# Where the finished batch's last operations, the bounds' check, the heads of attn2 and the first embedding sums stand in a two-layer attention kernel

## The chip, the core and the metric

The kernel runs on one core of a Trainium2 chip. The metric is device time in microseconds (us) of one execution; three executions of the kernel before gave 2773.93, 2775.44 and 2777.14 us, so the median is 2775.44 us. The engines are named as the profile names them: PE is the matrix engine (TensorE), DVE the vector engine, ACT the scalar engine, POOL is GpSimd, and SP is the sync engine, which here does nothing but issue DMAs.

## What is computed

Everything is float32. The input x has shape (2, 512, 64, 32): two batches of 2048 tokens (S) with 512 channels (C).

```
# layer 0: attention with 8 heads of 64; q and k also see a position embedding
q, k = concat(x, emb) @ Wq, concat(x, emb) @ Wk      # emb: 32 rows of (h), 32 rows of (w)
v    = x @ Wv
x    = x + softmax(q k^T / 8) v @ Wout + bout
# layer 1: Nystrom attention, 256 landmarks (means of 8 tokens), on the normalised tokens
t = tokens(x);  q, k, v = norm(t) @ Wqkv
attn1 = softmax(q kL^T); attn2 = softmax(qL kL^T); attn3 = softmax(qL k^T)
Z   = pinv(attn2)                                     # 6 iterations
t   = t + (attn1 (Z (attn3 v)) + conv33(v)) @ Wout1 + bout1
# feed-forward: two linear maps, folded in the kernel into one 512x512 map mT
t   = t + norm(t) @ mT
```

The kernel computes softmax without subtracting a maximum, which is safe while every score stays under a bound. It therefore also computes bounds of the scores (`bound`, 128 x 24) and, from them, a flag `bad`; if the flag is set, a general path runs after the fast one. With these inputs only the fast path runs.

## The kernel before, in words

PE, DVE, ACT and POOL each run their instructions in the order in which the program writes them (`manual_schedule`, for these four engines). An instruction that waits holds up everything behind it on its engine. The DMA queue of SP is not in this list: a scheduler orders it. So the order in the Python text is the schedule, and where PE would wait, other work is woven in by Python generators. A generator does one unit of work and then yields; `advance(list)` (L792 on) takes one unit from the first generator of a list; a unit that yields `GAP` makes `advance` pass on, so that a gap is a call in which that generator gives PE nothing more.

**Start (L820 to L855, L857 on).** The weights and x are loaded; 20 matmuls warm PE up (L847). For each pair of heads (`Heads0`, 4 pairs for each batch) the embedding's part of q (and of k) is one small matmul (L880), copied by DVE (L882) and spread by one POOL addition to a tile `e` of 128 x 2048 (L884). Each of the four token blocks of 512 is then projected by four matmuls (L896) and added to `e` by DVE (L899). Projections use two PSUM banks in turn (tag `pp`).

**Layer 0 (to about 1430 us).** Attention of pair after pair, with the next pair's projections as filler.

**Between the layers (about 1430 to 1755 us).** Layer 0's output of batch 1 is finished (`out0`, `norm0`), while the keys, queries and landmarks of layer 1 are made for batch 0 and then for batch 1 (`others`, `keys_and_queries`, L1230 to L1255). Between them stands, for each pair of heads, `attend` (attn2: matmuls L1271, exponential L1278 on ACT, normalisation L1282 to L1288 on DVE) and `gram` (L1298). For the first three pairs, `attend` takes one PSUM tile of two banks for both heads, `scs`, and gives head h the half `scs[:, h, :]`; from the fourth pair on it takes a bank for each head. `start_scale` (L1178 on) makes a number from all attn2 for the inversion, with a reduction across partitions on POOL.

**The pair loop (about 1755 to 2600 us).** `todo` holds the eight pairs, those of batch 1 first (n = 0 to 3), then those of batch 0 (n = 4 to 7). For pair n, `pinv` runs five iterations; each has two squarings of M and two of R, one for each head (flip L1513, copied by ACT L1514; products L1523; DVE sums L1536). After iteration c it calls `chunk(c)`: attn1 of the pair before (scores L1580, exponential L1585, sum L1589, values L1596, row sums L778, reciprocal L1609; the reciprocals are spread to rows by eight DMAs, L789; `attn1_end`, L1616 on DVE and L1617 on POOL, takes them up in the next chunk), attn3 of the pair after, and, between, `advance(finish)`. Then three small products follow, each a chain from PE (L1498) to ACT (L1502) to PE (L1507) to DVE (L1536), and `last(i)`, i = 0 to 5, fills the holes in these chains. All values matmuls of attn1 write one PSUM bank (tag `av1`), which `attn1_end` reads.

**The finished batch's end (`finish1_units`).** Once batch 1 has all its heads, its four token blocks t go through `Finish1`: load of the block x1 (four DMAs, L1628), four `out` units (four matmuls L956, residual sum L963 on DVE), the normalisation (`norm_units`, `statistics`), and four `map` units (L1673; DVE L1662, L1663; DMA to the output). The normalisation's steps are: sums of channels (DVE L974, L975); mean on PE (L978) and subtraction (DVE L979, 128 x 2048); squares (three ACT instructions, L982, L985) and their sums (three DVE instructions, L987, L988); variance on PE (L991), square root (ACT L993) and reciprocal (DVE L1641). The block's tile `xr` exists once: the next block's load waits for the output DMAs of the block before. In the kernel before, the generator is put into `finish` after pair 4, and so is first advanced in pair 5:

```
        pair.pinv(chunk, last)
        if n == NPAIR:
            finish.append(finish1_units(1, [p.o for p in todo[:NPAIR]]))
```

**The end (about 2600 us on).** attn1 of pair 7 (`last_attn1`) and what is left of `finish` are woven with the first units of batch 0's own four blocks by a string, one letter a unit: f advances `finish`, 1 is attn1, a and b the `out` units of blocks 0 and 1, s and t their normalisations. Then come the bounds' check, and the four blocks' maps, which take the banks `av1`, `pr`, `av3`, `pr`:

```
    for c in "f1f1f1f1f1f1f1fa1a1a1as11bs1bs1bbt":
...
    todo[-1].attn1_end(NTB - 1)
    drain(outs[1])
    next(st[0])
```

The check is one matmul (L2049) with a matrix `halves` (three POOL memsets, L2045 to L2047, in one of three row buffers, tag `rinv`), three small DVE instructions (L2051 to L2054) and a reduction on POOL (L2055). The tiles for batch 0's own blocks (`fs`, loads L1628) take the buffers in which the heads' outputs `o` of batch 1 stood (tag `qo`).

Of the kernel before, what the change touches and what calls it, by code (L numbers as in the profile page):

```python
# [663 lines left out]
def fast_path(  # L664
# [145 lines left out]
    def gap(n=1):  # L810
        for _ in range(n):
            yield GAP
# [5 lines left out]


    emb_sb = wpool0.tile([64, H + W], F32, name="emb_f")  # L820
    nc.vector.memset(emb_sb, 0.0)
    w_sb = {kind: wpool0.tile([P, KC, C], F32, name=f"w{kind}_f") for kind in "qk"}
    we = {kind: wpool0.tile([64, C], F32, name=f"we{kind}_f") for kind in "qk"}

    def load_w0(kind, cols, queue=nc.sync):
        w = {"q": wq0, "k": wk0}[kind]
        nc.sync.dma_start(w_sb[kind][:, :, cols], chunked(w[:C, cols]))
        queue.dma_start(we[kind][:, cols], w[C:, cols])

    nc.gpsimd.dma_start(emb_sb[:32, :H], freq)  # L830
    nc.gpsimd.dma_start(emb_sb[32:, H:], time)
    load_w0("q", slice(0, P), nc.scalar)

    def load_x(src, b, name, first=0, n=NTB):
        tiles = []
# [21 lines left out]
    class Heads0:  # L857
# [13 lines left out]
        def embedded_and_projected(self, kind):  # L871

            cols, xbs = self.cols, self.xbs
            if kind == "q":
                self.q = qopool.tile([P, S], F32, tag="qo", name=f"q_{self.name}")

            def embedded(kind):

                fp = bank(f"fp_{kind}_{self.name}")
                nc.tensor.matmul(fp[:, : H + W], lhsT=we[kind][:, cols], rhs=emb_sb, start=True, stop=True)  # L880
                ft = wpool0.tile([P, H + W], F32, tag="ft", name=f"ft_{kind}_{self.name}")
                nc.vector.tensor_copy(ft, fp[:, : H + W])  # L882
                e = wpool0.tile([P, H, W], F32, tag="e", name=f"e_{kind}_{self.name}")
                nc.gpsimd.tensor_tensor(  # L884
                    e,
                    ft[:, :H].unsqueeze(2).to_broadcast([P, H, W]),
                    ft[:, H:].unsqueeze(1).to_broadcast([P, H, W]),
                    ALU.add,
                )
                return e.rearrange("p h w -> p (h w)")  # L890

            def project(kind, dst, e, t):
                toks = slice(t * TB, (t + 1) * TB)
                pp = bank(f"pp_{kind}_{self.name}_{t}")
                for k in range(KC):
                    nc.tensor.matmul(  # L896
                        pp, lhsT=w_sb[kind][:, k, cols], rhs=xbs[t][:, k, :], start=k == 0, stop=k == KC - 1
                    )
                nc.vector.tensor_tensor(dst[:, toks], pp, e[:, toks], ALU.add)  # L899

            dst = self.q if kind == "q" else self.k
            e = embedded(kind)
            yield
            yield GAP
            for t in range(NTB):
                project(kind, dst, e, t)
                yield
# [60 lines left out]
    def deviation(name):  # L968
        return apool.tile([P, TB], F32, tag="rstd", name=f"rstd_{name}", bufs=1)

    def statistics(xb, xn, part, name, squares, row):


        nc.vector.tensor_tensor(part, xb[:, :2, :], xb[:, 2:, :], ALU.add)  # L974
        nc.vector.tensor_tensor(part[:, 0, :], part[:, 0, :], part[:, 1, :], ALU.add)  # L975
        yield
        mean = bank(f"mean_{name}")
        nc.tensor.matmul(mean, lhsT=mean_w, rhs=part[:, 0, :], start=True, stop=True)  # L978
        nc.vector.tensor_tensor(xn, xb, mean.unsqueeze(1).to_broadcast([P, KC, TB]), ALU.subtract)  # L979
        yield  # L980
        sq, *others = squares()
        nc.scalar.activation(sq, xn[:, :2, :], AF.Square)  # L982
        n = 2 // len(others)
        for i, other in enumerate(others):
            nc.scalar.activation(other, xn[:, 2 + i * n : 2 + (i + 1) * n, :], AF.Square)  # L985
            to = sq[:, i * n : (i + 1) * n, :]
            nc.vector.tensor_tensor(to, to, other, ALU.add)  # L987
        nc.vector.tensor_tensor(sq[:, 0, :], sq[:, 0, :], sq[:, 1, :], ALU.add)  # L988
        yield
        var = bank(f"var_{name}")  # L990
        nc.tensor.matmul(var, lhsT=mean_w, rhs=sq[:, 0, :], start=True, stop=True)  # L991
        rstd = row()
        nc.scalar.activation(rstd, var, AF.Sqrt, bias=eps, scale=1.0)  # L993
        yield rstd
# [204 lines left out]
    class Pair:  # L1199
# [59 lines left out]
        def attend(self):  # L1259

            i, L = self.i, self.L
            scs = scores_bank(f"sc2_{i}") if i + 1 < NPAIR else None
            X = self.X = [zpool.tile([P, 2, LM + 1], F32, tag=f"M{h}", name=f"X_{i}_{h}") for h in range(2)]
            rs = small.tile([P, 4], F32, tag="rs2", name=f"rs2_{i}")
            for h in range(2):
                nc.gpsimd.memset(X[h][:, :, LM:], 1.0)
            for h in range(2):
                rows_h = slice(h * D, (h + 1) * D)
                sc = scs[:, h, :] if scs is not None else bank(f"sc2_{i}_{h}")
                for t in range(2):  # L1270
                    nc.tensor.matmul(  # L1271
                        sc[:, t * LM : (t + 1) * LM],
                        lhsT=L[0][rows_h, t * P : (t + 1) * P],
                        rhs=L[1][rows_h, :],
                        start=True,
                        stop=True,
                    )
                nc.scalar.activation(X[h][:, :, :LM], sc.rearrange("p (t n) -> p t n", n=LM), AF.Exp)  # L1278
# [340 lines left out]
    class Finish1:  # L1619
# [10 lines left out]
        def out_units(self):  # L1630
            return residual_units(self.b, self.t, self.xb, self.os, wo_sb, b1_sb, self.name)

        def steps(self, row):
            def squares():
                sq = apool.tile([P, 2, TB], F32, tag="acc", name=f"sq_{self.name}")
                return sq, *(row_of(f"sq{k}_{self.name}").unsqueeze(1) for k in (2, 3))

            self.xn = self.xn()
            for rstd in statistics(self.xb, self.xn, self.xn[:, :2, :], self.name, squares, row):
                if rstd is not None:  # L1640
                    nc.vector.reciprocal(rstd, rstd)  # L1641
                    self.rstd = rstd
                yield

        def norm_units(self):
            steps = self.steps(lambda: deviation(self.name))
            next(steps)
            yield GAP
            next(steps)
            yield  # L1650
            next(steps)
            yield from gap(2)
            next(steps)
            yield
# [28 lines left out]
    def finish1_units(b, os):  # L1683
        for t in range(NTB):
            xb = block_of(lpool, "xr", f"xb_g_{b}_{t}")
            f = Finish1(b, t, os, xb, lambda: block_of(lpool, "xn", f"xn_g_{b}_{t}"))
            yield from f.out_units()
            yield from f.norm_units()
            yield from f.map_units(lambda m, name: bank(name))
# [184 lines left out]
            next(first, None)  # L1874
    drain(first)
    todo[1].prefetch_w()
    vals = [values(1)]
    advance(vals)
    for n in todo[NPAIR - 1].front():
        advance(vals, n // 2)  # L1880
    start_scale()
    todo[0].prefetch1(kvpool.tile([P, S], F32, tag="k", name="q2_first"))


# [2 lines left out]
    for n, pair in enumerate(todo):  # L1887
# [20 lines left out]
        def chunk(c):  # L1908
            nonlocal landmarks
            if before and 0 < c <= n_ones:  # L1910
                before.attn1_end(c - 1)
            advance(finish)
            if c == NTB:
                if after:
# [64 lines left out]
        landmarks = start = None  # L1979
        n_ones = NTB if n + 2 < len(todo) else NTB - 1  # L1980
        pair.pinv(chunk, last)
        if n == NPAIR:
            finish.append(finish1_units(1, [p.o for p in todo[:NPAIR]]))

    def last_attn1():
        pair, ended = todo[-1], []
        for t in range(NTB):
            for j in range(2 if t else 0):
                pair.attn1_scores(t, j)
                if ended:  # L1990
                    pair.attn1_end(ended.pop())
                yield
            pair.attn1_add(t)
            pair.attn1_values(t)
            yield
            pair.attn1_sums(t)
# [31 lines left out]
    st = [f.steps(deviation_of(t)) for t, f in enumerate(fs)]  # L2028

    ones_last = last_attn1()  # L2030
    for c in "f1f1f1f1f1f1f1fa1a1a1as11bs1bs1bbt":
        if c == "f":
            advance(finish)
        else:
# [3 lines left out]
    todo[-1].attn1_end(NTB - 1)  # L2038
    drain(outs[1])
    next(st[0])  # L2040

    n = 3 * B * NPAIR

    halves = row_of("halves_f")[:, :P]
    nc.gpsimd.memset(halves, 0.0)  # L2045
    nc.gpsimd.memset(halves[:D, :D], 1.0)
    nc.gpsimd.memset(halves[D:, D:], 1.0)  # L2047
    bp = bank("bp_f")
    nc.tensor.matmul(bp[:, :n], lhsT=halves, rhs=bound, start=True, stop=True)  # L2049
    ok = small.tile([P, n], F32, name="ok_f")  # L2050
    nc.vector.tensor_scalar(ok, bp[:, :n], SAFE, None, ALU.is_lt)  # L2051
    oks = small.tile([P, 1], F32, name="oks_f")
    nc.vector.tensor_reduce(oks, ok, AX.X, ALU.min)
    nc.vector.tensor_scalar(oks, oks, -1.0, 1.0, ALU.mult, ALU.add)  # L2054
    nc.gpsimd.partition_all_reduce(bad, oks, P, bass_isa.ReduceOp.max)  # L2055

    for t in range(NTB):
        maps = fs[t].map_units(wide_banks, 1 if t + 1 < NTB else 2)
        if t + 1 < NTB:
# [96 lines left out]
```

## Time and profile before

| What | us |
|---|---|
| median of three runs | 2775.44 |
| the profiled execution, its own time | 2775.64 |
| its span, first to last instruction | 2773.8 |
| PE busy | 2712.4 |
| DVE busy | 1638.7 |
| ACT busy | 905.8 |
| POOL busy | 197.2 |
| 1400 to 1580 us: span, PE busy | 180.0, 173.0 |
| 2222 to 2604 us: span, PE busy | 382.0, 364.7 |
| 2604 to 2677 us: span, PE busy | 73.0, 62.2 |

The profile covers one execution. Its page gives each engine's busy time, and other views list the instructions in order of time with the idle time ahead of them and what ended it ("<-"). Lines of code stand as L and a number. A line of a view in order of time begins with the start and the length of a group of like instructions. The share of the TensorE clock that was granted is recorded apart; in most of the span it is 1, and in eight stretches within it 0.5.

### The profile page before, as it was taken

Reading aid. Unit: us, or ns where it says so; the run is one execution under the profiler, and the core shown is the slowest. Engines: PE = TensorE matmul, PEld = TensorE weight load, DVE = VectorE, ACT = ScalarE, POOL = GpSimd, SP = SyncE. Lnnn points to the kernel's source line nnn. Section 1 sums busy time; section 2 is a strip of 40 time slices with the busy share of each in tenths; the row PEclk is TensorE's granted clock in tenths of the full one; section 3 lists DMA queues with packets and bytes.
Section 4 is the critical chain, followed back from the end, with each engine's and each line's share of the span. In section 5 each row is a group of like instructions: output and inputs, shape, how many; then the busy total and the mean of one; then the engine's idle time right before and its main releaser. Section 6 shows DMA issues by size and latency. Waiting matters only on the chain. (4 is left out here: it accounts for less than half of the span.)

```text
span 2773.8 us, 41257 instructions
## 1 busy us (share of the span) xinstructions
PE 2712.4 (98%) x17010; PEld 1365.7 (49%) x17010; DVE 1638.7 (59%) x2076; ACT 905.8 (33%) x1352; POOL 197.2 (7%) x133
## 2 busy tenths in 40 slices
PE   9999999999999999999999999999999999999898
PEld 5343443434343334343344455777677766555334
DVE  3768787774557765747657444544644545556455
ACT  1344343433335244435412223233332323221210
POOL 1101101010001200100002000000000000000000
PEclk9999999999999999999999999999999999999999
DMA  3000000201111200012025532313111202111301
GB/s 115 12 9 9 13 6 7 69 24 50 32 50 54 80 9 7 8 49 64 24 87 186 201 118 92 97 34 115 54 36 58 81 9 90 38 66 31 106 32 47
DMA packets 110358, 157.22 MB, mean 57 GB/s; under 512 B 16065, under 2 KB 67793, under 8 KB 107601
## 3 DMA queue, kind: packets, MB, share of 16 engines
q1 hardware_dynamic: 105664, 137.68, 15.7%
q0 software_dynamic: 4416, 16.79, 1.6%
q8 instruction: 135, 2.21, 0.4%
q14 instruction: 63, 0.51, 0.1%
q10 hardware_dynamic: 80, 0.03, 0.0%
HBM read 82.48 MB, written 55.19 MB: 50 GB/s over the span
## 5 line engine op out<-in xcount | busy, mean ns | idle before, releaser
L1075 DVE TENSOR_TENSOR acc_f<-acc_f,p_f 128x1024 f32<-128x1024 f32 x448 | 589.4, 1316 | 235.6 <-ACT p_f L1065 207.0
L1065 ACT ACTIVATE p_f<-sc_f 128x1024 f32<-128x1024 f32 x512 | 496.4, 1021 | 561.9 <-PE sc_f L1057 550.4
L1057 PE MATMUL sc_f<-q_f,k_f 64*64 64x512 f32 x4096 | 491.7, 595 | 2.4 <-ACT p_f L1065 2.4
L1087 PE MATMUL av_f<-p_f,v_f 64*64 64x512 f32 x4096 | 484.3, 589 | 0.0
L1087 PEld LDWEIGHTS av_f<-p_f,v_f 64*64 64x64 f32 x4096 | 156.5, 133 | 283.0 <-issue 283.0
L1057 PEld LDWEIGHTS sc_f<-q_f,k_f 64*64 64x64 f32 x4096 | 144.8, 133 | 280.9 <-issue 256.0
L1230 PE MATMUL pp<-xh,w 128*128 128x512 f32 x512 | 233.0, 608 | 0.7 <-ACT q L1233 0.7
L1230 PEld LDWEIGHTS pp<-xh,w 128*128 128x128 f32 x512 | 96.5, 194 | 123.2 <-issue 116.0
L1523 PE MATMUL pb<-R 128*128 128x192 f32 (+1 forms) x640 | 151.4, 383 | 1.6 <-DVE M L1536 1.6
L1523 PE MATMUL pa<-M 128*128 128x192 f32 (+1 forms) x640 | 150.6, 380 | 0.0
L941 PEld LDWEIGHTS vp_f<-wv_f,x 128*128 128x128 f32 x1024 | 115.6, 192 | 12.7 <-issue 11.0
L941 PE MATMUL vp<-w,xh 128*128 128x128 f32 x1024 | 120.8, 276 | 0.0
L941 PEld LDWEIGHTS vp<-w,xh 128*128 128x128 f32 x1024 | 117.0, 192 | 7.2 <-issue 4.2
L1523 PEld LDWEIGHTS pb<-R 128*128 128x128 f32 x640 | 107.8, 192 | 25.2 <-DVE M L1536 2.3
L896 PE MATMUL pp_q_f<-x,wq_f 128*128 128x512 f32 x256 | 115.9, 606 | 2.9 <-DMA x<-in_x_dram 1.5
L941 PE MATMUL vp_f<-wv_f,x 128*128 128x128 f32 x1024 | 118.5, 276 | 0.0
L1523 PEld LDWEIGHTS pa<-M 128*128 128x128 f32 x640 | 108.0, 193 | 21.0 <-ACT M L1514 2.5
L956 PE MATMUL yp_g<-o,wo_f 128*128 128x512 f32 x256 | 115.5, 598 | 0.8 <-DVE y_g L1662 0.8
L956 PE MATMUL yp_f<-q_f,wo_f 128*128 128x512 f32 x256 | 114.0, 598 | 2.2 <-issue 1.2
L1673 PE MATMUL fp_g<-xn_g,mT 128*128 128x512 f32 (+1 forms) x264 | 115.7, 589 | 0.0
L896 PE MATMUL pp_k_f<-x,wk_f 128*128 128x512 f32 x256 | 114.1, 599 | 0.4 <-DVE q_f L899 0.4
L1105 POOL TENSOR_TENSOR q_f<-q_f,rinv_f 128x512 f32<-128x512 f32 x32 | 45.9, 1434 | 920.4 <-DMA rinv_f<-acc_f 920.4
(196 smaller groups left out, 2762.0 us busy)
## 6 DMA issues: line engine op xcount, KB each, us to landing
xh<-xh_fd SPq DMA_DIRECT2D x12, 1024.0 KB, 5.4
rinv_f<-acc_f SPq DMA_DIRECT2D x256, 32.0 KB, 1.9
xr_f<-in_x_dram SPq DMA_DIRECT2D x8, 1024.0 KB, 5.2
x_fd<-xr_f POOLq DMA_DIRECT2D x8, 1024.0 KB, 4.6
xh_fd<-xn_f POOLq DMA_DIRECT2D x8, 1024.0 KB, 4.6
k_fd<-k SPq DMA_DIRECT2D x32, 256.0 KB, 2.8
q_fd<-q SPq DMA_DIRECT2D x32, 256.0 KB, 2.9
xb_g<-x_fd SPq DMA_DIRECT2D x32, 256.0 KB, 4.3
```

The source lines that it names most:

```text
L896: nc.tensor.matmul(pp, lhsT=w_sb[kind][:, k, cols], rhs=xbs[t][:, k, :], start=k == 0, stop=k == KC - 1)
L941: nc.tensor.matmul(vp[:, j * P : (j + 1) * P], lhsT=xb[:, k, j * P : (j + 1) * P], rhs=w_of(k), start=k == 0, stop=k == KC - 1,)
L956: nc.tensor.matmul(yp, lhsT=wo_sb[:, k, m * P : (m + 1) * P], rhs=oTs[k][:, toks], start=k == 0, stop=k == NPAIR - 1,)
L1057: nc.tensor.matmul(sc[r * D : (r + 1) * D, h, :], lhsT=hd.k[rows, lo : lo + D], rhs=hd.q[rows, t * TB : (t + 1) * TB], start=True, stop=True,)
L1065: nc.scalar.activation(p, sc, AF.Exp, scale=D**-0.5)
L1075: nc.vector.tensor_tensor(acc, first if c == 1 else acc, p, ALU.add)
L1087: nc.tensor.matmul(av[r][half, :], lhsT=hd.v[keys, c, half], rhs=pp[keys, h, :], start=c == 0, stop=c == NST - 1,)
L1105: nc.gpsimd.tensor_tensor(o, o, rinv, ALU.mult)
L1230: nc.tensor.matmul(pp, lhsT=self.w[j][:, c, :], rhs=xhs[t][:, c, :], start=c == 0, stop=c == KC - 1)
L1523: nc.tensor.matmul(dst, lhsT=lhsT[:, k, t * P : (t + 1) * P], rhs=rhs[:, k, :], start=k == 0, stop=k == 1)
L1673: nc.tensor.matmul(fp[:, cols], lhsT=mT[:, k, m * P : (m + 1) * P], rhs=self.xn[:, k, cols], start=k == 0, stop=k == KC - 1,)
```

## The change

It has six parts.

1. The queue of a first weight's DMA becomes that of its caller, so that the first columns of Wq and their embedding rows go out from ACT's queue, followed there by the two embedding tables, which POOL's queue issued before. The memset of the table's tile covers only the two blocks that no DMA fills. The embedding sums of the very first pair (q and k) run on DVE.
2. `statistics` can stop between the squares (ACT) and their sums (DVE): `apart`. The finished batch's `norm_units` use it, and place their gaps differently; each block also begins with two gaps after its load.
3. The finished batch's generator is put into `finish` in pair 4, chunk 1.
4. `attend` takes a buffer of its own for each head of the first three pairs, and its memsets of the ones column run on DVE.
5. The string of the last stage is another, and `last_attn1` adds its exponentials one unit earlier.
6. The bounds' check stands ahead of and around `start_scale`, between the layers.

```diff
-    nc.vector.memset(emb_sb, 0.0)
+    nc.vector.memset(emb_sb[:32, H:], 0.0)
+    nc.vector.memset(emb_sb[32:, :H], 0.0)
...
-        nc.sync.dma_start(w_sb[kind][:, :, cols], chunked(w[:C, cols]))
+        queue.dma_start(w_sb[kind][:, :, cols], chunked(w[:C, cols]))
         queue.dma_start(we[kind][:, cols], w[C:, cols])
-    nc.gpsimd.dma_start(emb_sb[:32, :H], freq)
-    nc.gpsimd.dma_start(emb_sb[32:, H:], time)
     load_w0("q", slice(0, P), nc.scalar)
+    nc.scalar.dma_start(emb_sb[:32, :H], freq)
+    nc.scalar.dma_start(emb_sb[32:, H:], time)
...
-                nc.gpsimd.tensor_tensor(
+                engine = nc.gpsimd if self.b or self.hp else nc.vector
+                engine.tensor_tensor(
                     e,
...
-    def statistics(xb, xn, part, name, squares, row):
+    def statistics(xb, xn, part, name, squares, row, apart=False):
...
             nc.scalar.activation(other, xn[:, 2 + i * n : 2 + (i + 1) * n, :], AF.Square)
+        if apart:
+            yield
+        for i, other in enumerate(others):
             to = sq[:, i * n : (i + 1) * n, :]
             nc.vector.tensor_tensor(to, to, other, ALU.add)
...
-            scs = scores_bank(f"sc2_{i}") if i + 1 < NPAIR else None
+            scs = [scores_bank(f"sc2_{i}_{h}")[:, 0, :] for h in range(2)] if i + 1 < NPAIR else None
...
-                nc.gpsimd.memset(X[h][:, :, LM:], 1.0)
+                nc.vector.memset(X[h][:, :, LM:], 1.0)
...
-                sc = scs[:, h, :] if scs is not None else bank(f"sc2_{i}_{h}")
+                sc = scs[h] if scs else bank(f"sc2_{i}_{h}")
...
         def norm_units(self):
-            steps = self.steps(lambda: deviation(self.name))
+            steps = self.steps(lambda: deviation(self.name), True)
+            next(steps)
+            yield from gap(2)
+            next(steps)
+            yield
             next(steps)
             yield GAP
-            next(steps)
-            yield
             next(steps)
             yield from gap(2)
             next(steps)
...
             f = Finish1(b, t, os, xb, lambda: block_of(lpool, "xn", f"xn_g_{b}_{t}"))
+            yield from gap(2)
             yield from f.out_units()
...
+    halves = row_of("halves_f")[:, :P]
+    nc.gpsimd.memset(halves, 0.0)
+    nc.gpsimd.memset(halves[:D, :D], 1.0)
+    nc.gpsimd.memset(halves[D:, D:], 1.0)
     vals = [values(1)]
     advance(vals)
     for n in todo[NPAIR - 1].front():
         advance(vals, n // 2)
+    n_bounds = 3 * B * NPAIR
+    bp = bank("bp_f")
+    nc.tensor.matmul(bp[:, :n_bounds], lhsT=halves, rhs=bound, start=True, stop=True)
+    ok = small.tile([P, n_bounds], F32, name="ok_f")
+    nc.vector.tensor_scalar(ok, bp[:, :n_bounds], SAFE, None, ALU.is_lt)
...
     start_scale()
+    nc.gpsimd.partition_all_reduce(bad, oks, P, bass_isa.ReduceOp.max)
...
                 before.attn1_end(c - 1)
+            if n == NPAIR and c == 1:
+                finish.append(finish1_units(1, [p.o for p in todo[:NPAIR]]))
             advance(finish)
...
-        if n == NPAIR:
-            finish.append(finish1_units(1, [p.o for p in todo[:NPAIR]]))
...
         pair, ended = todo[-1], []
+        pair.attn1_add(0)
...
                     pair.attn1_end(ended.pop())
+                if j:
+                    pair.attn1_add(t)
                 yield
-            pair.attn1_add(t)
             pair.attn1_values(t)
...
-    for c in "f1f1f1f1f1f1f1fa1a1a1as11bs1bs1bbt":
+    for c in "11fff11f1ff1aaffff1f1f1f1faas11bs1bs1bbt":
...
-    halves = row_of("halves_f")[:, :P]
...
-    nc.gpsimd.partition_all_reduce(bad, oks, P, bass_isa.ReduceOp.max)
```

More of the change, by code (lines that the diff above doesn't have):

```diff
@@ L1631, in out_units, with steps @@
             return residual_units(self.b, self.t, self.xb, self.os, wo_sb, b1_sb, self.name)
-        def steps(self, row):
+        def steps(self, row, apart=False):
             def squares():
@@ L1638, in steps @@
             self.xn = self.xn()
-            for rstd in statistics(self.xb, self.xn, self.xn[:, :2, :], self.name, squares, row):
+            for rstd in statistics(self.xb, self.xn, self.xn[:, :2, :], self.name, squares, row, apart):
                 if rstd is not None:
@@ L1880, in fast_path @@
         advance(vals, n // 2)
+    n_bounds = 3 * B * NPAIR
[3 more added lines that the diff above has]
+    nc.vector.tensor_scalar(ok, bp[:, :n_bounds], SAFE, None, ALU.is_lt)
+    oks = small.tile([P, 1], F32, name="oks_f")
+    nc.vector.tensor_reduce(oks, ok, AX.X, ALU.min)
+    nc.vector.tensor_scalar(oks, oks, -1.0, 1.0, ALU.mult, ALU.add)
     start_scale()
+    nc.gpsimd.partition_all_reduce(bad, oks, P, bass_isa.ReduceOp.max)
     todo[0].prefetch1(kvpool.tile([P, S], F32, tag="k", name="q2_first"))
@@ L2040, in fast_path @@
     next(st[0])
-    n = 3 * B * NPAIR
-    halves = row_of("halves_f")[:, :P]
[L2045 to L2054, printed above, removed]
-    nc.gpsimd.partition_all_reduce(bad, oks, P, bass_isa.ReduceOp.max)
     for t in range(NTB):
```

## The prediction

> **What bounds the kernel.** The page's first part comes first.
>
> ```profile
> PE 2712.4 (98%) x17010; PEld 1365.7 (49%) x17010; DVE 1638.7 (59%) x2076; ACT 905.8 (33%) x1352; POOL 197.2 (7%) x133
> ```
>
> PE is busy in all but 61.4 us of the span of 2773.8. The change takes no matmul away, so it can win only idle time of PE and matmuls that ran slowly. The view of waits, for PE, names the idle time:
>
> ```profile
> PE p_pb L1513 <- DVE R L1536: 6.9, 2, 6.3
> PE sc L1271 <- ACT X L1278: 6.2, 3, 3.5
> PE rs L778 <- DVE acc L1589: 5.1, 1, 5.1
> PE bp_f L2049 <- POOL halves_f L2047: 4.9, 1, 4.9
> PE mean_g L978 <- DVE xn_g L975: 3.2, 1, 3.2
> PE pp_q_f L896 <- DVE q_f L899: 0.9, 1, 0.9
> ```
>
> The columns are total, times and longest, in us. The second line is attn2, the fourth the bounds' check, the first, third and fifth the finished batch. Next, PE in order of time around attn2 of pair 1 and of pair 3:
>
> ```profile
> 1500.80 1.13 PE L1271 MATMUL sc<-L,L 64*128 64x256 f32 x4
> 1505.40 1.13 PE L1271 MATMUL sc<-L,L 64*128 64x256 f32 x4 [3.47 <-ACT X L1278]
> 1506.46 5.36 PE L1230 MATMUL pp<-xh,w 128*128 128x512 f32 x8
> ...
> 1577.66 1.14 PE L1271 MATMUL sc<-L,L 64*128 64x256 f32 x8
> ```
>
> The second head's matmuls wait until ACT has taken the first head's exponential. Pair 3 has a bank a head, and its eight take 1.14 us without a wait. The eight projections behind the wait take 5.36 us, against 3.70 for the same eight at 1440.78: the view of windows shows why.
>
> ```profile
> 1506.40:1509.80 3.40, 3.40 (x5) 1.51 (x5) 3.33 (x6) 0.60 (x1) 0.86 (x3) 0.50 0.64 242
> 1578.80:1582.00 3.20, 3.20 (x9) 1.52 (x9) 2.93 (x6) 1.09 (x2) 0.00 (x0) 1.00 0.73 251
> ```
>
> The last column but two is the granted clock: 0.50 behind the wait, 1.00 behind pair 3. So a long wait is paid twice. Last, the largest gap, and DVE at the end:
>
> ```profile
> 2402.74 0.48 PE L1513 MATMUL p_pb<-ident,R 128*128 128x128 f32 x1 [6.32 <-DVE R L1536]
> 2403.67 3.78 PE L1523 MATMUL pb<-R 128*128 128x192 f32 x8 [0.45 <-DVE M L1536]
> ```
> ```profile
> 2401.54 0.75 DVE L963 SCALAR_TENSOR_TENSOR xb_g<-yp_g,b_f,xb_g 128x512 f32<-128x512 f32 x1 [9.94 <-DMA xb_g<-x_fd]
> ...
> 2674.10 0.69 DVE L1616 TENSOR_TENSOR rinv<-av,rinv 128x512 f32<-128x512 f32 x1 [0.36 <-DMA rinv<-acc]
> ```
>
> The inversion's matmul waits for DVE, which stands at a residual sum of the finished batch until its block lands.
>
> **What the Trainium skill says.** "TensorE: Matmul & The Clock Gate", Part 1: the clock halves when a free-running window of 3413 ns was idle, and a busy one restores it. The trace agrees in length (slow stretches of 3.4 or 6.8 us, each behind waits), but not that a whole idle window is needed: 0.74 us of visible wait at 1433.6 did it. "GPSIMD Engine Reference", 4.1: two-input sums are about twice as slow as on VectorE. Here POOL's `e` takes 3.62 us and DVE's L979, of the same 128 x 2048, 2.28. "ScalarE: Activation LUTs", What ACT_TABLE_LOAD costs: 1283 ns and a drain; the trace has 1.28 us and shows no drain. "Trainium Kernel Development and Optimization", Key Constraints: queues of several engines share the DMA engines, so spreading issues saves only issue time.
>
> **The parts.**
>
> *Start.* PE ends its warm-up at 7.43 us and starts the embedding at 7.36, so earlier tables win nothing. `e` of q ends at 16.74 on POOL; on DVE it follows the copy at 8.12 and ends at about 10.4, ahead of the first projection (11.45). The 0.94 us wait at 16.59 goes. The 0.40 at 25.05 stays (a bank waits for DVE's 0.69 us drain), and so does most of the 1.46 us wait for x, whose issue moves up by one issue (0.44 us), past nothing else on SP. POOL's queue loses two issues, ACT's gains three ahead of a table load that nothing needs before 43 us. Gain **1.0** (bounds -1.0, if tables on ACT's queue, one 0.5 us issue after another, land after 7.4, since wek took 6.5 us to land, and 1.5).
>
> *attn2.* From first matmul to next projection, the three pairs take 2.93 us (1431.74 to 1434.67), 5.66 and 4.36; pair 3 takes 1.07. Pair 0 saves 1.86 and its slow stretch 1.70 (5.40 - 3.70); pair 2 3.29 and 1.49 (8.62 - 7.13). In pair 1 something else is late: the variance, at 1511.66, needs DVE's sum L988, which ends at 1509.15 in a DVE stream without idle time since 1498. PE would be there at 1505.5. It starts at 1509.3 with the two memsets (0.1 us each on POOL) now on DVE, after a wait of 3.7, and I let a slow stretch (1.7) follow: gain 0.6. Sum **8.9** (5.2 if all stretches stay, 10.6 if none does). Behind the memsets on DVE stand only sums that wait for ACT.
>
> *Bounds' check.* It leaves a wait of 4.95 us. But the next matmul, the first map, writes bank `av1`, which DVE's L1616 reads until 2674.79, waiting for spread DMAs: PE starts at 2674.85 instead of 2677.01. The matmul itself (0.3) is paid earlier, behind `gram` at 1751.6; DVE's three instructions (0.12 + 0.18 + 0.15) delay `start_scale` by 0.5, inside the 3.4 us by which M is ready (1755.25) before PE wants it (1758.62); without that cover they would cost 0.5. The POOL reduction queues behind `start_scale`'s own; POOL has nothing urgent. Gain **1.9** (0 to 3.5). The slow stretch behind this wait (now 3.0) stays.
>
> *Finished batch.* I wrote out every call of `finish` for both kernels: 53 calls before, 69 after, 14 of them in the last string instead of 8. Waits that belong to it, in order of PE: 1.05 (2331.7), 6.32, 0.45, 1.59, 0.26, 0.63, 0.59, 3.24, 0.59, 0.46, 1.06, 0.53, 0.55, 5.06 and 0.78 (2637.2), sum 23.2. After the change:
> - Load of block 1: it is issued in pair 5 with two gaps, and 14 us of PE work ahead of the first sum that needs it, against 2.5 + 3.6 us for output DMA and load. 6.32 and 0.45 go.
> - Mean and squares of block 0 fall at the end of pair 4. DVE's 2.28 us subtraction now precedes `iteration_start`, and ACT's squares (1.06 + 0.61 + 0.61) precede the flip copy of pair 5's first product: the flip copy starts 3.6 us after the scores end, against 1.1 in the trace (2231.87, 2232.97). New wait **2.5**.
> - Variance of block 0, in pair 5 chunk 2: square root, table load back and reciprocal (0.69 + 1.28 on ACT, 3.35 on DVE) lie beside 7 us of scores and values. Nothing.
> - Squares of block 1, pair 6 chunk 3, ahead of a flip copy: 0.4. The chain waits of pairs 5 and 6 (1.05, 1.59, 0.26) go, since maps fill them.
> - Block 2: its load still lands after its first product in pair 7 chunk 0, as now: 1.3. Its mean no longer waits (3.24 goes); products wait for banks 0.35; in chunk 3, without matmuls, its sums (2.07) and the row sums' DMA hold DVE: 1.5.
> - Pair 7's end: 0.46 stays; the third small product has no filler: 0.55.
> - Last string: values of block 1 wait for `av1` (row DMAs, DVE behind L974): 1.4. The variance of block 3 comes straight after two `out` units: residual sum 0.75 and sums 2.07 make 2.9. The row sums of block 0 no longer stand behind squares: 5.06 goes; 0.4 for the rest. 0.78 goes.
> Sum 11.8, gain 11.4. Slow stretches before cost 2.2 (behind 6.32), 2.9 (behind 3.24) and 1.5 (behind 5.06), by the matmuls' excess over like ones; one of 1.7 comes behind the 2.9. Gain 4.9, together **16.3** (9 to 22: waits of 15 and no clock gain less one stretch, or waits of 7 and no stretch).
> Buffers: `sq` is held over two chunks, so sums of attn1 take the other `acc` tile; its spread landed some 19 us earlier (about 2397, 2416). No cost. SP carries the same DMAs; the 16 loads of the last blocks (7.2 us) now wait for `out` units in the string, behind block 0's spread and ahead of block 1's.
>
> **Sum:** 1.0 + 8.9 + 1.9 + 16.3 = 28.1. The profiled execution took 2775.64 (span 2773.8 and 1.8 around it), 0.2 above the median: 2775.44 - 28.1 gives **2747**. About 0.2% (5.5 us) is what a measurement can tell from no change.
>
> **Rivals.**
> - *SP's order* (15%). If those 16 loads are queued ahead of block 0's spread, `av1` comes free 7.2 + 3.5 us later, 11 us, and a slow stretch, 1.7: gain 15.4, **2760**. For it: at 2390 a spread already delayed an output DMA by 4 us. Against: the spread is ready 5 us before the loads.
> - *attn2 gains nothing* (10%): the second head waits not for the shared tile but for ACT's order. Then 8.9 is lost: **2756**. Against it speaks pair 3.
> - *Slower* (9%): DVE and ACT in the pair loop. The 16 normalisation steps of the four blocks stand in order ahead of the inversion's small copies and sums. Now they cost 1.0 each (1.05, 1.59, 0.26, 3.24, 0.59, 5.06, 2.9, 1.5, over 16); I count 0.6 (2.5, 0.4, 0.35, 1.5, 2.9, 1.7). From 2.4 each on (0.6 + 28.1/16) the kernel is slower, from 2.7 on by over 0.2%; at 3.0, half of what 3.24 and its stretch cost, it is **2786**. For it: gaps give such steps no PE work. Against: most chunks have 8 us of other matmuls. At 2.0 to 2.7 it is no change (6%).
>
> **Chances.** Forecast 60%, the others 10, 15, 6 and 9%. Faster 85% (60 + 10 + 15), same 6%, slower 9%. The forecast's own bounds give 2737.6 (gain 1.5 + 10.6 + 3.5 + 22) to 2762.2 (-1.0, 5.2, 0, 9); both rivals on the fast side lie within. All terms at their best is unlikely, so the range is **2739 to 2763**, with some 80%.
>
> **What would show it.** Right: attn2's L1271 as one group of 8 in 1.1 us three times, and clock 1 behind pairs 0 and 2; a wait of about 3.7 at the variance behind pair 1; first map waiting about 3 us for L1616; no wait over 3 us between 2300 and 2600; new waits at the start of pair 5 (flip copy) and at block 3's variance. PE idle time falls from 61 to about 45 us. Wrong: several new waits of over 2 us with slow stretches in pairs 4 to 6, DVE or ACT named; or block 0's spread behind loads on SP.

## The result, and the profile after

The changed kernel takes 2767.59 us, the median of 8 executions (2763.43 to 2769.79); beside it, on the same chip, the kernel before took 2774.51 (8 executions, 2773.41 to 2777.14). The ratio is 0.9974, with a 95% interval of 0.9964 to 0.9984: a gain of 4 to 10 us, not of 28. The forecast was 2747 and its range ended at 2763.

The profiled execution after took 2768.05 us, with a span of 2766.2. In the program text everything has moved by a few lines: L1271 is now L1277, L1596 is L1602, L1616 is L1622, L956 is L959, L1628 is L1634, L1673 is L1681, and the loop's L1513 and L1536 are L1519 and L1542.

The page's first part, of the kernel after:

```profile
PE 2705.5 (98%) x17010; PEld 1362.3 (49%) x17010; DVE 1643.3 (59%) x2095; ACT 906.2 (33%) x1352; POOL 188.5 (7%) x113
```

PE is busy for 6.9 us less with the same 17010 matmuls, so that much comes from matmuls that ran at the full clock. Its idle time, 60.7 us, has hardly moved from 61.4. So idle time that the change took away has come back elsewhere. The view of PE's waits says where (total, times, longest, in us):

```profile
PE av L1602 <- DVE rinv L1622: 13.7, 1, 13.7
PE var_n L997 <- issue: 3.7, 1, 3.7
...
PE fp_g L1681 <- DVE rinv L1622: 3.2, 1, 3.2
PE p_pb L1519 <- DVE R L1542: 3.0, 2, 1.9
PE var_g L997 <- DVE sq_g L994: 2.9, 1, 2.9
...
PE pa L1529 <- ACT M L1520: 1.4, 1, 1.4
...
PE p_pa L1519 <- DVE M L1493: 1.2, 1, 1.2
```

The lines of 6.2, 5.1 and 4.9 us that the prediction showed are gone; of those of 6.9 and 3.2, 3.0 and 0.8 are left. The second, third, fifth and sixth of the lines above are waits that it named (3.7, about 3, 2.9 and 2.5). The first is a single wait of 13.7 us that its sum doesn't have. PE around it, in order of time:

```profile
2588.63 2.04 PE L1586 MATMUL sc<-q,L 64*128 64x512 f32 x8
2604.41 3.68 PE L1602 MATMUL av<-p,u 128*64 128x512 f32 x8 [13.75 <-DVE rinv L1622]
2608.03 1.54 PE L981 MATMUL mean_g<-xn_g,mean_w 128*128 128x512 f32 x2
```

The values' matmul of block 1 in the last string waits until DVE has read the bank of block 0. Behind it the matmuls are slow too: eight in 3.68 us, which take 1.94 at the full clock. DVE, in the same stretch:

```profile
2590.78 0.69 DVE L978 TENSOR_TENSOR xn_g<-xn_g 128x512 f32<-128x512 f32 x1
2603.58 0.69 DVE L1622 TENSOR_TENSOR rinv<-av,rinv 128x512 f32<-128x512 f32 x1 [12.10 <-DMA rinv<-acc]
```

DVE isn't late: it has nothing to do for 12.10 us and waits for the DMAs that spread block 0's reciprocals. So the next view is SP's queue:

```profile
2583.89 3.04 SPq L789 DMA_DIRECT2D rinv<-acc  x5
2587.03 9.60 SPq L1634 DMA_DIRECT2D xb_g<-x_fd  x16
2596.99 2.60 SPq L789 DMA_DIRECT2D rinv<-acc  x3
```

SP issues five of the eight spread DMAs, then the 16 loads of the last four blocks, 0.6 us each, and only then the other three. PE stands still for three small issues. The kernel before had the same loads and no such cut:

```profile
2593.31 1.27 SPq L1628 DMA_DIRECT2D xb_g<-x_fd  x3
2595.07 5.01 SPq L789 DMA_DIRECT2D rinv<-acc  x8
2600.13 7.66 SPq L1628 DMA_DIRECT2D xb_g<-x_fd  x13
```

There it was the loads that were cut in two, and a spread in one piece. For the kernel after, the view of windows agrees (busy us of PE, PEld, DVE, ACT and POOL with instructions in brackets, granted clock, DMA share, GB/s):

```profile
2590.67:2604.42 13.75, 0.01 (x1) 0.04 (x2) 1.62 (x4) 1.19 (x3) 0.02 (x1) 0.67 0.78 265
2604.40:2609.00 4.60, 4.59 (x10) 1.35 (x10) 1.00 (x1) 0.00 (x0) 2.12 (x1) 0.51 0.00 2
```

In the first line PE does nothing, DVE and ACT work for under 2 us each, and the DMA engines are at 0.78: it doesn't tell whether the spread waited for its turn on SP or for a share of DMA engines full of the loads' 4 MB. In the second line the clock is at half.

The attn2 part, by contrast, looks as forecast (PE, pair 0 and pair 1):

```profile
1431.23 1.14 PE L1277 MATMUL sc<-L,L 64*128 64x256 f32 x8
1432.30 3.70 PE L1236 MATMUL pp<-xh,w 128*128 128x512 f32 x8
...
1497.18 1.14 PE L1277 MATMUL sc<-L,L 64*128 64x256 f32 x8
1498.25 3.70 PE L1236 MATMUL pp<-xh,w 128*128 128x512 f32 x8
1505.64 1.31 PE L997 MATMUL var_n<-xr_f,mean_w 128*128 128x512 f32 x2 [3.69 <-issue]
1506.74 5.12 PE L1236 MATMUL pp<-xh,w 128*128 128x512 f32 x8
```

Both heads go as one group of eight, eight projections behind pair 0 take 3.70 us, and behind pair 1 the variance waits 3.69 us, with a slow stretch after it.

### The profile page after: what moved, and what is told of

The parts are those of the page before. It is cut to its first block, busy times and chain, and to the rows that moved or that the text cites. A ratio compares the mean times of both kernels' runs of the same rounds, so it can differ in the third digit from the quotient of the medians.

```text
span 2766.2 us, 41210 instructions
## 1 busy us (share of the span) xinstructions
PE 2705.5 (98%) x17010; PEld 1362.3 (49%) x17010; DVE 1643.3 (59%) x2095; ACT 906.2 (33%) x1352; POOL 188.5 (7%) x113
## 4 chain that ended last, share of the span: by engine, by line
PE 89%; DVE 6%; DMA 2%; ACT 1%; issue 1%; SPq 1%; ACTq 0%; DVEq 0%; POOL 0%; POOLq 0%
PE sc_f L1063 15%; PE av_f L1093 14%; PE pp L1236 8%; PE pb L1529 5%; PE pa L1529 4%; PE vp_f L944 4%; PE vp L944 4%; PE fp_g L1681 4%; PE pp_k_f L899 4%; PE pp_q_f L899 4%; PE yp_g L959 3%; PE yp_f L959 3%; DVE acc_f L1081 2%; PE sc L1358 2%; PE sc L1586 2%; PE av L1602 2%
## 5 line engine op out<-in xcount | busy, mean ns | idle before, releaser
L1681 PE MATMUL fp_g<-xn_g,mT 128*128 128x512 f32 (+1 forms) x264 | 115.9, 589 | 3.2 <-DVE rinv L1622 3.2
L959 PE MATMUL yp_f<-q_f,wo_f 128*128 128x512 f32 x256 | 113.8, 598 | 2.2 <-issue 1.2
L959 PE MATMUL yp_g<-o,wo_f 128*128 128x512 f32 x256 | 114.7, 597 | 0.0
```

What stands on the lines that cost most here:

```text
L959: nc.tensor.matmul(yp, lhsT=wo_sb[:, k, m * P : (m + 1) * P], rhs=oTs[k][:, toks], start=k == 0, stop=k == NPAIR - 1,)
L1681: nc.tensor.matmul(fp[:, cols], lhsT=mT[:, k, m * P : (m + 1) * P], rhs=self.xn[:, k, cols], start=k == 0, stop=k == KC - 1,)
```

## The experiments

The theory: the three parts other than the finished batch's are worth what the prediction said, and the finished batch's gain was eaten by SP's order, which cuts block 0's spread in two. The rivals: the bytes of the loads hold up the spread wherever it is queued; the finished batch's new order costs as much by its own small waits; attn2 or the bounds' check fell short. All medians below are of five or more executions (e9: four), each beside the kernel before on the same chip, whose median was 2774.0 to 2774.3 us in these runs.

**e1: the loads behind the spread.** The blocks' objects, which issue the loads when they are made, are made two units later (`L` in the string makes one):

```diff
-    fs = [last_block(t) for t in range(NTB)]
...
+    def load_block():
+        f = last_block(len(fs))
...
-    for c in "11fff11f1ff1aaffff1f1f1f1faas11bs1bs1bbt":
+    for c in "11LLLLfff11f1ff1aaffff1f1f1f1faas11bs1bs1bbt":
```

> The changed kernel with one difference: the 16 loads of the last four blocks are issued two units later in the program, so that SP queues all 8 spread DMAs of block 0's row sums, then the 16 loads. Nothing else moves on any engine. Theory 1 (SP's order): the wait of 13.75 us at the values' matmul, at 2590.7 in the changed kernel, falls to about 1.4 us, and the slow stretch behind it (the first four values' matmuls 3.68 us instead of 1.94) goes: 13 to 14 us less than the changed kernel's 2767.6, about 2754. Rival (the bytes of the loads, 4 MB, slow the spread's DMAs wherever they stand, or the wait only moves to the residual sums that need the loads): a wait of over 8 us stays between 2585 and 2640, and the time is within 4 us of 2767.6.

Measured: 2753.8 us (2750.26 to 2758.06), ratio 0.9927 (0.9913 to 0.9941). SP's queue and PE in the profile of e1:

```profile
2569.84 17.36 SPq L789 DMA_DIRECT2D rinv<-acc  x15
2587.30 9.35 SPq L1634 DMA_DIRECT2D xb_g<-x_fd  x16
```
```profile
2590.59 1.94 PE L1602 MATMUL av<-p,u 128*64 128x512 f32 x8 [1.56 <-DVE rinv L1622]
...
2604.08 1.36 PE L997 MATMUL var_g<-sq_g,mean_w 128*128 128x512 f32 x2 [2.86 <-DVE sq_g L994]
```

The spread is in one piece (one group here with seven of the spread before it), the wait is 1.56 us, close to the 1.4 of the prediction, and the matmuls behind it run in 1.94 us. The place of 16 issues in SP's list is worth 13.8 us between the medians, half of the whole forecast gain.

**e2: attn2 alone** on the kernel before:

```diff
-            scs = scores_bank(f"sc2_{i}") if i + 1 < NPAIR else None
+            scs = [scores_bank(f"sc2_{i}_{h}")[:, 0, :] for h in range(2)] if i + 1 < NPAIR else None
...
-                nc.gpsimd.memset(X[h][:, :, LM:], 1.0)
+                nc.vector.memset(X[h][:, :, LM:], 1.0)
...
-                sc = scs[:, h, :] if scs is not None else bank(f"sc2_{i}_{h}")
+                sc = scs[h] if scs else bank(f"sc2_{i}_{h}")
```

> The kernel before with attn2's part of the change alone (a bank for each head's scores, the memsets of X on DVE). Theory 1 (the prediction's term): 8.9 us less than before, about 2765.6; PE goes from pair 0's and pair 2's second heads without a wait, and a wait of about 3.7 us for the variance follows pair 1. Rival (attn2 waits for ACT's order, not for the shared tile): within 1 us of before, 2774.5.

Measured: 2765.85 us (2764.67 to 2769.02), ratio 0.9973 (0.9962 to 0.9983): 8.2 us less, against 8.9 forecast. The rival is out. In its profile the wait at L1271 is gone and PE's wait for the variance is there, as 3.69 us.

**e3: the finished batch's part alone** (parts 2, 3 and 5 of the change) on the kernel before.

```diff
...
+            if n == NPAIR and c == 1:
+                finish.append(finish1_units(1, [p.o for p in todo[:NPAIR]]))
...
-    for c in "f1f1f1f1f1f1f1fa1a1a1as11bs1bs1bbt":
+    for c in "11fff11f1ff1aaffff1f1f1f1faas11bs1bs1bbt":
```

> The kernel before with the finished batch's part alone (its load a gap earlier, its squares' sums apart, its start within pair 5's chunks, the order of the last string). The other parts measured so far on the changed kernel's trace take 1.5 us off at the start, 8.7 at attn2 and about 2 at the bounds' check. Theory 1 (this part is worth nothing, since the wait of 13.75 us for the split spread eats what the pair loop won): 2773 to 2779, no gain. Rival (the part wins its 16.3 us as predicted and something else in the sum lost it): about 2758.

Measured: 2778.41 us (2775.22 to 2784.54), ratio 1.0018 (1.0012 to 1.0025): this part, forecast to win 16.3, loses 4.4. Its waits:

```profile
PE av L1599 <- DVE rinv L1619: 13.7, 1, 13.7
```

It is the same wait (this kernel has the lines at L1599 and L1619), so it doesn't come from the parts' meeting.

**e4: start and bounds' check alone** (parts 1 and 6).

```diff
...
-    nc.gpsimd.dma_start(emb_sb[:32, :H], freq)
...
+    nc.scalar.dma_start(emb_sb[:32, :H], freq)
...
     start_scale()
+    nc.gpsimd.partition_all_reduce(bad, oks, P, bass_isa.ReduceOp.max)
```

> The kernel before with the start (tables on ACT's queue, first embedding sums on VectorE) and the bounds' check (moved to the middle of the kernel) alone. Theory 1 (the prediction's terms 1.0 and 1.9): 2.9 us less than before, about 2771.6. Rival (the slow stretch at the first small products is longer with the new start, as in the changed kernel's trace, where it took 6.8 us instead of 3.4, and gives the start's gain back): 0 to 1.5 us less, about 2773.5.

Measured: 2771.71 us (2769.01 to 2776.67), ratio 0.9992 (0.9985 to 0.9999): 2.3 us less, against 2.9 forecast. The interval (0.3 to 4.2 us) doesn't separate the two expectations, and no run separates the start from the bounds' check. The rival's longer slow stretch isn't in this kernel's profile: behind the wait near 921 us the clock stays at 1.

**e8: everything but the finished batch's part** (parts 1, 4 and 6).

> The changed kernel without the finished batch's part: start, attn2 and bounds' check on the kernel before. Theory 1 (the parts add up): 8.2 (attn2 alone, 2774.0 - 2765.85) and 2.3 (start and bounds' check alone) less than before, about 2763.5, which is 4 us less than the whole change: the finished batch's part costs 4. Rival (the parts depend on each other, the attn2 gain falls at the end where the finished batch's new order is needed to keep it): 2766 to 2770, no less than the whole change.

Measured: 2762.65 us (2761.57 to 2764.23), ratio 0.9957 (0.9944 to 0.9971). The parts add up, and the change is some 5 us slower than the same change without its largest part.

**e5: half of the loads ahead.** As e1, but the first two blocks are made where the changed kernel makes all four:

```diff
+    load_block()
+    load_block()
-    for c in "11LLLLfff11f1ff1aaffff1f1f1f1faas11bs1bs1bbt":
+    for c in "11LLfff11f1ff1aaffff1f1f1f1faas11bs1bs1bbt":
```

> Between the changed kernel and e1: SP queues 5 spread DMAs of block 0, then 8 of the 16 loads (blocks 0 and 1), then the last 3 spread DMAs, then the other 8 loads. Theory 1 (each load queued ahead costs its turn on SP, 9.6 us for 16, 0.6 each): the wait at the values' matmul is 13.75 - 8 * 0.6 = about 8.9 us, the slow stretch behind it stays, and the time is 4 to 6 us below the changed kernel's 2767.6, about 2762.5. Rival (it's not the number of loads but that the group of 8 is cut in two, or the landing of one load): the wait stays at 12 to 14 us and the time within 2 us of 2767.6.

Measured: 2760.66 us (2760.36 to 2764.64), ratio 0.9956 (0.9942 to 0.9969). SP's queue and PE:

```profile
2584.18 3.89 SPq L1634 DMA_DIRECT2D xb_g<-x_fd  x8
2588.12 1.78 SPq L789 DMA_DIRECT2D rinv<-acc  x3
2590.02 5.17 SPq L1634 DMA_DIRECT2D xb_g<-x_fd  x8
```
```profile
2595.11 3.68 PE L1602 MATMUL av<-p,u 128*64 128x512 f32 x8 [7.29 <-DVE rinv L1622]
```

The wait follows the number of loads ahead of the three issues: 1.56 us with none, 7.29 with 8, 13.75 with 16. The expectation of 8.9 took 0.6 us for a load; these eight took 0.49 each, the other eight 0.65.

**e7: the loads on another queue**, at the changed kernel's place in the program:

```diff
-                nc.sync.dma_start(xb[:, m, :], chunked(x1_d[b])[:, m, toks])
+                queue = nc.sync if b else nc.gpsimd
+                queue.dma_start(xb[:, m, :], chunked(x1_d[b])[:, m, toks])
```

> The changed kernel with the 16 loads of the last four blocks on GpSimd's DMA queue, issued at the same place in the program; SP then has the 8 spread DMAs of block 0 in one piece, while the same 4 MB move at the same time. Theory 1 (SP's order): the wait falls from 13.75 to 1.4 to 4 us, and the time is 2752 to 2757. Rival (the bytes: 4 MB on the DMA engines hold up the spread's small packets wherever they are queued): the wait stays over 8 us and the time over 2762.

Measured: 2756.14 us (2754.8 to 2759.19), ratio 0.994 (0.9926 to 0.9954). PE:

```profile
2591.81 3.35 PE L1602 MATMUL av<-p,u 128*64 128x512 f32 x8 [3.08 <-DVE rinv L1622]
```
```profile
2590.97 0.69 DVE L1622 TENSOR_TENSOR rinv<-av,rinv 128x512 f32<-128x512 f32 x1 [1.43 <-DMA rinv<-acc]
```

With the same bytes on the way and SP free, 3.08 us are left, and DVE waits 1.43 us for the spread's DMAs; in e1 it doesn't wait for them at all. So the 12.2 us between 13.75 and 1.56 can be divided. From the start of the spread's first issue to the end of its last, SP takes 15.7 us in the changed kernel and 4.9 in e1 (and in e7): 10.8 us are SP's list. From the last issue to DVE's start it is 4.0 us against 2.6 in e1 (4.1 in e7): the other 1.4 are a slower landing beside the loads. e5 has the same form: 5.7 us over e1, 3.9 of them issues.

**e6: e1 with block 3's sums of squares between the two output units:**

```diff
-    for c in "11LLLLfff11f1ff1aaffff1f1f1f1faas11bs1bs1bbt":
+    for c in "11LLLLfff11f1ff1afafff1f1f1f1faas11bs1bs1bbt":
```

> e1 (the loads behind block 0's spread) with one letter of the last string moved: the step that sums block 3's squares on VectorE comes between the last blocks' two output units instead of behind both. Theory 1 (the wait of 2.86 us for block 3's variance comes from the second residual sum, 0.75 us, and the sums, 2.07, standing one behind the other on VectorE): the wait falls to under 0.5 us, and with it the slow stretch behind it goes (1 to 1.7 us): 2.5 to 4.5 us below e1's 2753.8, about 2750. Rival (the sums then stand ahead of a residual sum or a row sum that another matmul wants): the wait turns up 3 to 15 us away with over 2 us, and the time is within 1 us of e1.

Measured: 2752.72 us (2748.75 to 2754.75), ratio 0.9922 (0.9908 to 0.9936). Against e1's 2753.8 with a spread of 8 us this isn't told apart. PE in its profile:

```profile
2602.16 1.10 PE L997 MATMUL var_g<-sq_g,mean_w 128*128 128x512 f32 x2 [1.51 <-DVE sq_g L994]
...
2652.80 3.67 PE L1681 MATMUL fp_g<-xn_g,mT 128*128 128x512 f32 x8 [3.16 <-DVE rinv L1622]
```

The variance waits 1.51 us instead of 2.86: little more than half of the fall that was expected, though nothing of it turns up elsewhere as a long wait. The expectation under 0.5 was wrong.

**e9: e6 with the banks of the last blocks' maps exchanged:**

```diff
-        return product_bank(name) if m % 2 else side_bank(1 + m, name)
+        return side_bank(m, name) if m % 2 else product_bank(name)
```

> e6 with the PSUM banks of the last blocks' four maps exchanged: the first and third write the two product banks, the second and fourth the values' banks. The order of instructions is the same on every engine. Theory 1 (as the prediction's part on the bounds' check had it: the first map waits 3.16 us only for the bank that VectorE's L1622 still reads): the wait falls to under 1 us and the time is about 3 us below e6's 2752.7, about 2749.7. Rival (the first map, or what follows it, waits for something else that comes no earlier, such as the mean of the next block or VectorE's 3.35 us reciprocal): at least 2.5 us of wait stay between the variance and the fifth map, and the time is within 1 us of e6.

Measured: 2745.2 us (2742.82 to 2748.18), ratio 0.9897 (0.9882 to 0.9913), the fastest of all and ahead of both kernels. PE:

```profile
2646.11 1.02 PE L997 MATMUL var_g<-sq_g,mean_w 128*128 128x512 f32 x2
2646.97 3.60 PE L1681 MATMUL fp_g<-xn_g,mT 128*128 128x512 f32 x8
```

The first map follows the variance at once: the wait of 3.16 us was for the bank alone, as the prediction's part on the bounds' check had it. The gain over e6 is 7.5 us between medians, 4 more than that wait. In the two profiles, which are 6.3 us apart, what goes beyond the wait lies in slow stretches of e6 at 924 and 2487 us, where both kernels are the same and e9 has none. Where the waits ahead of them fall against the clock's windows differs between the two executions (last section), so this part is luck there. A slow stretch behind the first map's wait, as e1's profile has it, could be a part of the 4 that the banks do win; no run shows how much.

## Why the prediction was wrong, point by point

| Part | forecast gain, us | measured alone, us |
|---|---|---|
| start and bounds' check | 2.9 | 2.3 (e4) |
| attn2 | 8.9 | 8.2 (e2) |
| finished batch | 16.3 | -4.4 (e3) |
| sum | 28.1 | 6.1; whole change 6.9 |

*Attn2* was right in mechanism, places and size: pairs 0 and 2 without a wait or slow stretch, the variance of pair 1 next late (3.7 forecast, 3.69 measured).

*Start and bounds' check* were right, together, within what was measured. The first map's wait for L1622 came as named: 3.16 us for 4.95.

*Finished batch: the step that failed* is its last sentence: "SP carries the same DMAs; the 16 loads of the last blocks (7.2 us) now wait for `out` units in the string, behind block 0's spread and ahead of block 1's", costed at nothing. That the loads wait for an `out` unit is right: in the kernel before, the first load goes out 1.06 us after the start of the last such unit (2592.25 and 2593.31), and in e8 1.06 us as well. What is wrong is "behind block 0's spread". The rival *SP's order* had against it that the spread is ready 5 us before the loads. In the kernel after, that `out` unit starts at 2585.11, only 1.2 us after the spread's first issue (2583.89), and the first load goes out 3.1 us after that issue, while eight issues of a spread take 5.0. The loads stand ahead of the string in the text, and SP's list has them inside block 0's spread; when e1 and e5 move them in the text, the list follows. In the term, "values of block 1 wait for `av1` ...: 1.4" became 13.75; e1 gives 1.56 when only that order is mended. This is 13.8 of the missed 20.6 us. The rival named it and priced the wait at 11 us more and one slow stretch; measured, 12.2 more, with the clock at half for 13.7 us, in only 4.5 of which PE works. It gave 2760 and not 2767.6, because it kept the rest of the ledger. The last sign of being wrong that the prediction gave, the spread behind loads on SP, is the one that came.

*The rest of this term* is too small as well. e1 against e8 gives the part, with its order mended, as 8.9 us (2762.65 - 2753.8), not 16.3. (Nor does the range's low end, 9, follow: waits of 15 leave 8.2 of the 23.2 before a stretch is taken off.) By the profiles, PE's waits between the fourth pair's first product (2037.8 us before, 2027.4 in e1) and the first last-block map, bounds' check and first map apart, are 23.6 us before and 17.1 in e1, against 11.8 forecast; that is 5 us of the shortfall. PE's busy time in that stretch falls by 2.0 us, where 4.9 were forecast for slow stretches; that is the other 3. Sources of some 4 of the 5:
- Waits that I hadn't counted, in e1: 0.68 (scores at 2235.3), 0.36 and 1.20 (2323.3, 2359.7), 0.75 (2519.8, a mean that was to wait no longer) and 1.04 (2571.6). For the 1.20, the residual sum of the last output unit stands on DVE ahead of the first step of the inversion.
- Waits that came larger: pair 7 chunk 3, forecast 1.5, took 1.88 and 0.60; pair 7 chunk 0, forecast 1.3, took 1.14 and 0.59.
- One that came smaller: the flip copy of pair 5's first product, forecast 2.5, took 1.44.

The chunk 3 wait in the kernel after, PE and DVE:

```profile
2537.93 0.33 PE L1519 MATMUL p_pb<-ident,R 128*128 128x128 f32 x1 [1.88 <-DVE R L1542]
2538.86 1.46 PE L1529 MATMUL pb<-R 128*128 128x192 f32 x6 [0.60 <-DVE M L1542]
```
```profile
2533.79 0.69 DVE L1622 TENSOR_TENSOR rinv<-av,rinv 128x512 f32<-128x512 f32 x1 [0.63 <-DMA rinv<-acc]
2534.40 2.35 DVE L993 TENSOR_TENSOR sq_g<-sq_g,sq_g 128x512 f32<-128x512 f32 x2
2536.79 0.69 DVE L994 TENSOR_TENSOR sq_g<-sq_g 128x512 f32<-128x512 f32 x1
```

DVE stands 0.63 us for the row sums' DMAs, then needs 2.35 + 0.69 for sums that the prediction took at 2.07, and only then the product's sums. These small waits are read from the traces; no run took one of them away. The rival *slower* rested on such waits; at 5 us more over the 16 steps they cost 0.3 each more than forecast, far from the 1.8 more that it needed.

"No wait over 3 us between 2300 and 2600" and "idle time falls to about 45 us" were the tests that failed; with SP's order mended, e1 meets the first and has 47.8 us.

## What to carry to other kernels

When work is reordered, follow the DMA issues too, in the order of the queue that carries them and not of the text: three small DMAs behind 16 loads held PE up for 13.75 us. A forecast of "behind A and ahead of B" on a queue that a scheduler orders is an open term, and its price, the issue time of everything that could come between, belongs in the likeliest case. After such a change measure its parts alone: here a part that loses 4 us was hidden in a whole that wins 7.

## What the hardware showed that was not expected

*When the clock halves.* The slow stretches are 3.4, 6.8 or 13.7 us long. In each of the eleven profiles, all their edges lie on one grid with steps of 3413 ns. This fits the free-running window of 3413 ns that the Trainium skill gives in "TensorE: Matmul & The Clock Gate", Part 1. But the page asks for an idle window, and here less was enough. From 45 us to 8 us before the end, a window at full clock in which PE had no matmul for 2.02 us or more was followed by a slow one 43 times of 43, and only 10 of the 43 were idle throughout. With 1.6 to 2.0 us of idle time it was 6 of 28, and with less 2 of 8566 (0.74 us both). A slow window was followed by another when PE was idle in it for 0.59 us or more (25 of 25), and by a fast one otherwise (51 of 51).

So it counts where a wait falls on the grid. The same wait of 2.83 us, near 921 us, stands in all eleven kernels. In five of them one window there has 2.19 to 2.49 us of idle time, and a slow stretch followed, of 6.8 us in two (after, e2) and of 3.4 in three (before, e3, e6). In six (e1, e4, e5, e7, e8, e9) the wait is divided between two windows, none with over 2.00 us, and the clock stayed at 1. Two windows of e6, then two of e9, in the columns of the view of windows above:

```profile
920.51:923.92 3.41, 1.15 (x3) 0.67 (x4) 2.77 (x3) 0.00 (x0) 0.38 (x1) 1.00 0.01 4
923.93:927.32 3.39, 3.39 (x5) 1.35 (x4) 2.29 (x1) 1.02 (x2) 0.00 (x0) 0.50 0.00 0
```
```profile
918.99:922.39 3.40, 1.58 (x4) 0.38 (x2) 3.40 (x1) 0.00 (x0) 2.54 (x1) 1.00 0.66 248
922.40:925.80 3.40, 2.39 (x6) 1.19 (x7) 2.75 (x4) 0.00 (x0) 0.00 (x0) 1.00 0.00 0
```

The waits of 3.47 to 3.69 us near 1500 had a slow stretch in all eleven (3.4 us in eight, 6.8 in three). The grid lies differently in each profile, so for a wait of about 1.6 to 4 us (twice 2.0) a forecast can't know whether a stretch follows; the upper end is an estimate from the 2.0 us above. Single executions of one kernel here differ by up to 9.3 us (e3), and the slowest of these has a mean granted clock of 0.991, the fastest 0.994.

*Loads beside small DMAs.* With the 16 loads (4 MB) on another queue at the same time, PE's wait for the spread was about 1.5 us longer than with the loads behind it (3.08 against 1.56 us, e7 and e1). What cost far more was their turn on the queue, 10.8 us in the kernel after.
